# Four graph layers on one core: how the two 8-head attention layers end, and what the stages behind them find ready

## The chip, the core and the metric

The kernel runs on one core of a Trainium2 chip. The core has a matrix engine (PE; its weight loads are listed apart as PEld), a vector engine (DVE), an activation engine (ACT), a general engine (POOL) and a queue engine (SP), and 16 DMA engines that all of them share. PE multiplies out of SBUF into PSUM; DVE and ACT take results from there. DMAs are issued by SP and POOL, a few by ACT, and each of these issues its transfers in its own order. The metric is the device time of one execution in microseconds, the median of the runs.

## What is computed

The input is a matrix `x` of 3327 nodes by 512 features and an adjacency matrix `adj` of 3327 by 3327. Four layers follow one another, each of the form `x = layernorm(x + layer(x, adj))`:

```python
def _L0_gnn_ref(h, adj, W, a):            # layer 0: 8 heads of 64
    Wh = jnp.einsum('ni,hio->hno', h, W)
    f1 = jnp.einsum('hno,ho->hn', Wh, a1)
    f2 = jnp.einsum('hno,ho->hn', Wh, a2)
    e = jax.nn.leaky_relu(f1[:, :, None] + f2[:, None, :], ALPHA)
    attention = jax.nn.softmax(jnp.where(adj[None] > 0, e, NEG_INF), axis=-1)
    h_prime = jnp.einsum('hnm,hmo->hno', attention, Wh)
    ...
def _L1_gnn_ref(X, A, W_nb, b_nb, W_line, b_line, neibor_num):   # layer 1: the first 64 neighbours
    Ab = A > 0
    keep = Ab & (jnp.cumsum(Ab.astype(jnp.int32), axis=1) <= neibor_num)
    cnt = keep.sum(axis=1, keepdims=True).astype(X.dtype)
    nb_mean = (keep.astype(X.dtype) @ X) / jnp.maximum(cnt, 1.0)
    xj = jax.nn.leaky_relu(nb_mean @ W_nb.T + b_nb)
    xi = jax.nn.leaky_relu(X @ W_line.T + b_line)
    return xi + jnp.where(cnt > 0, xj, jnp.zeros((), X.dtype))
```

Layer 2 is again an attention with 8 heads of 64, with an elu behind it, and layer 3 one with 4 heads of 128 and an elu. Layer 1 is called SAGE below.

## The kernel before

The nodes are 26 tiles of 128 rows. Everything that PE does stands in an order written by hand; the instructions of the other engines are ordered by a scheduler with priorities, apart from those that `tc.keep_in_program_order` pins. Tiles come from pools with a fixed number of buffers, so a new tile waits until the users of the old one in its buffer are done. The adjacency, as 0 and 1 in one byte each, stays in SBUF as `mask` for all layers.

**Projection.** For each tile, `project1` transposes x (L258, copied by ACT in L259 to xT) and `project2` multiplies it with the weights (pw, L268), scales the result on DVE (vt, L274) and stores it. In layer 0 this runs while the adjacency comes in (`raw`, made to `mask` in L593). `rows` (L356) loads one row of scores per head and repeats it over 128 partitions (rb); `mean` (L283) adds the row that nodes without neighbours use.

**Attention.** The 26 tiles of results are two halves of 13, and a half has four units of two heads each (of one head in layer 3). A unit goes over 26 tiles j of neighbours. For each j and head, DVE forms t of 128 by 1664 (L402), ACT a sigmoid y of it (L405), and PE multiplies t with the values vj (po, L425) and y with pieces of the denominators (pd, L377, issued in pairs by `den`, three j's behind). A unit's jobs are run in the next unit, one per j: `transposed` (L450) turns ob, the copy of po, by PE, ACT copies the result to hb (L457), and SP stores it to hd in DRAM. After the fourth unit of a half the pieces in pd are added up: four transposes on DVE to db (L486, L487), two reductions to red (L491), four stores to dd in DRAM (L495) in pieces of 32 bytes, one load back in another layout (pes, L498), and `finish_sums` (L501) forms the reciprocals `rec`. A second way (from L522) copies pd to db by ACT and DVE and lets PE add by 13 matmuls (`sums`, L533), with `reciprocals` behind it; before the change only the very last unit of the kernel uses it.

**Counts.** `count_jobs` counts each node's neighbours by PE during layer 0. Its step `none` copies the counts out of PSUM (ct, L629), adds them up (pn, L631), stores them to ctd, and marks the nodes without neighbours (nb, L635).

**Between the layers.** `finish_steps` loads a group of two tiles of h (hd) and of the residual input (xr), divides by the denominators, applies elu, adds, and takes the norm (`norm_rows`: square root on ACT L154, the scaled copy L161). The first group of the next stage is finished inside the attention's end, by `ending`. `sage` has two phases: first projections of each tile (transposes L682, pz L690, pi L693, results as three bf16 parts, two kept in SBUF as zs, the third stored to zd), then sums over neighbours: pk (L770) counts along the neighbours, starting from a carry (cy, L659, copied to PSUM in L762), kt (L774) is the mask cut at 64, and acc (L809) sums over 26 tiles times three parts, the third read back as zl. `third` holds layer 3, with its own projection in groups of two tiles.

## Time and profile before

The three runs took 3410.44, 3410.56 and 3414.77 us; the median is 3410.56. The profiled execution took 3407.9 us, its span is 3406.2.

| engine | busy us | share of the span | instructions |
|---|---|---|---|
| PE | 3262.8 | 96% | 18423 |
| DVE | 2695.3 | 79% | 2630 |
| ACT | 2351.4 | 69% | 2128 |
| POOL | 214.7 | 6% | 344 |

| stage, from the trace | us from the span's start |
|---|---|
| layer 0, projection (adjacency comes in) | 0 to 143 |
| layer 0, attention | 143 to 957 |
| SAGE, projections | 960 to 1180 |
| SAGE, sums over neighbours, projection of layer 2 | 1180 to 1772 |
| layer 2, attention | 1772 to 2562 |
| layer 3 | 2562 to 3406 |

A line of the timeline or of a group names the line of the code, the engine, the operation, what is written and what is read, and the number of instructions; in brackets it tells how long the engine stood idle before it and what ended the wait. A wait line names the waiting instruction, what released it, the sum in us, how often, and the longest. Matmuls are pipelined, so the time between the starts of two lines is a better measure than the busy time of one.

### The profile page before, as it was taken

How to read it: one execution, taken by the hardware profiler on the slowest of the kernel's cores; microseconds unless marked ns; L12 is line 12 of the kernel's file. 1: busy time of each engine (PE TensorE's matmuls, PEld its weight loads, DVE VectorE, ACT ScalarE, POOL GpSimd, SP SyncE). 2: the span in 40 equal slices, each digit the busy share in tenths (PEclk: the TensorE clock that was granted, in tenths of full speed). 3: DMA queues.
4: the chain of work that ended last, by engine and by line, in shares of the span. 5: the costliest groups of instructions: out<-in, count | busy, mean ns of one | idle time of the engine just before them, and what ended most of it. 6: DMA issues, size and time to landing. Idle time of an engine off the chain costs nothing.

```text
span 3406.2 us, 47019 instructions
## 1 busy us (share of the span) xinstructions
PE 3262.8 (96%) x18423; PEld 1631.0 (48%) x18423; DVE 2695.3 (79%) x2630; ACT 2351.4 (69%) x2128; POOL 214.7 (6%) x344
## 2 busy tenths in 40 slices
PE   8899999999989899999989999999997999999997
PEld 7544344444434345555544444444445754445453
DVE  5799999999967544444449999999997766668886
ACT  2388999999943233333338999899996755559885
POOL 3100000000010111111110000000001000000000
PEclk9899999999989999999999999999998999999998
DMA  9544111110143443333320111211107411122311
GB/s 372 214 127 123 52 49 53 42 49 28 38 123 128 116 111 87 90 85 85 85 81 26 41 50 48 56 44 47 35 25 225 169 41 42 41 51 79 95 42 48
DMA packets 313365, 284.65 MB, mean 84 GB/s; under 512 B 134253, under 2 KB 248631, under 8 KB 313144
## 3 DMA queue, kind: packets, MB, share of 16 engines
q1 hardware_dynamic: 280584, 170.27, 16.9%
q0 software_dynamic: 27040, 103.70, 9.5%
q10 hardware_dynamic: 5520, 7.69, 0.7%
q8 instruction: 145, 2.38, 0.3%
q14 instruction: 76, 0.62, 0.1%
HBM read 212.22 MB, written 69.35 MB: 83 GB/s over the span
## 4 chain that ended last, share of the span: by engine, by line
PE 79%; issue 7%; DVE 6%; DMA 4%; ACT 2%; POOL 0%; SPq 0%; ACTq 0%; POOLq 0%; DVEq 0%
PE po L425 49%; PE acc L809 9%; PE pd L377 7%; PE pw L268 5%; DVE t L402 4%; PE pz L690 3%; PE pi L693 3%; DMA raw<-in_adjT_dram 2%; ACT y L405 1%; PE pt L453 1%; DMA cy<-ctd 1%; PE pk L770 1%; PE pt L258 0%; PE pa L1022 0%; DVE mask L593 0%
## 5 line engine op out<-in xcount | busy, mean ns | idle before, releaser
L402 DVE SCALAR_TENSOR_TENSOR t<-rb,qc,mask 128x1664 f32<-128x1664 f32 x1040 | 1959.9, 1957 | 167.7 <-PE po L425 150.1
L405 ACT ACTIVATE y<-t,bi,sc 128x1664 fp8e4<-128x1664 f32 x1040 | 1771.1, 1766 | 317.3 <-PE pd L377 304.4
L425 PE MATMUL po<-t,vj 128*64 128x448 f32 (+3 forms) x8320 | 1924.6, 520 | 25.0 <-DVE t L402 22.3
L425 PEld LDWEIGHTS po<-t,vj 128*64 128x64 f32 (+1 forms) x8320 | 848.3, 148 | 978.2 <-issue 689.7
L809 PE MATMUL acc<-zs,kt 128*128 128x512 bf16 x1352 | 405.1, 382 | 0.0
L809 PEld LDWEIGHTS <-kt 128*128 128x128 fp8e4 x2028 | 199.1, 98 | 250.8 <-issue 9.5
L268 PE MATMUL pw<-wsb,xT 128*128 128x264 f32 (+1 forms) x1248 | 299.8, 395 | 9.2 <-DVE vt L274 7.5
L762 ACT CAST pk<-cy 128x512 f32<-128x512 bf16 x169 | 98.9, 587 | 294.5 <-DVE kt L774 251.1
L377 PE MATMUL pd<-y,sden 128*32 128x448 fp8e4 (+1 forms) x4160 | 259.4, 342 | 8.2 <-ACT y L405 8.2
L268 PEld LDWEIGHTS pw<-wsb,xT 128*128 128x128 f32 x1248 | 240.4, 196 | 53.4 <-issue 5.0
L809 PE MATMUL acc<-zl,kt 128*128 128x512 bf16 x676 | 257.8, 381 | 4.0 <-DMA zl<-zd 4.0
L774 DVE SCALAR_TENSOR_TENSOR kt<-pk,mask 128x512 fp8e4<-128x512 f32 x169 | 116.0, 687 | 99.7 <-PE pk L770 99.7
L377 PEld LDWEIGHTS <-sden 128*32 128x32 bf16 x4160 | 117.6, 96 | 160.3 <-issue 137.6
L274 DVE TENSOR_TENSOR vt<-pw,dc 128x256 f32<-128x256 f32 x156 | 59.0, 418 | 141.2 <-ACT dc L269 137.1
L356 POOL DMA_DIRECT2D rb<-r x40 | 21.9, 548 | 1617.0 <-DVE t L402 1604.5
L272 ACT COPY rc<-pw 128x8 f32<-128x8 f32 (+1 forms) x78 | 12.7, 163 | 138.7 <-PE pw L268 136.2
L690 PE MATMUL pz<-wn,xT 128*128 128x512 f32 x208 | 97.4, 613 | 10.1 <-ACT xT L684 10.1
L693 PE MATMUL pi<-wl,xT 128*128 128x512 f32 x208 | 93.5, 592 | 0.0
L659 POOL DMA_DIRECT2D cy<-ctd x91 | 67.9, 746 | 338.4 <-ACT pk L762 310.2
L782 DVE SCALAR_TENSOR_TENSOR y<-acc,cnt,bnb 128x512 f32<-128x512 f32 x26 | 19.5, 751 | 85.9 <-PE acc L809 85.9
L593 DVE TENSOR_SCALAR mask<-raw 128x832 fp8e4<-128x832 int32 (+2 forms) x90 | 53.1, 598 | 40.4 <-DMA raw<-in_adjT_dram 40.1
L154 ACT ACT_TABLE_LOAD x45 | 57.7, 1283 | 37.3 <-DVE mv L153 36.7
(177 smaller groups left out, 1661.6 us busy)
## 6 DMA issues: line engine op xcount, KB each, us to landing
vj<-v SPq DMA_DIRECT2D x312, 128.0 KB
rb<-r POOLq DMA_DIRECT2D x40, 832.0 KB, 4.6
raw<-in_adjT_dram SPq DMA_DIRECT2D x67, 416.0 KB
cy<-ctd POOLq DMA_DIRECT2D x78, 256.0 KB, 3.9
h<-hd SPq DMA_DIRECT2D x61, 256.0 KB
v<-vt SPq DMA_DIRECT2D x50, 256.0 KB
hd<-hb SPq DMA_DIRECT2D x48, 256.0 KB
xr<-x POOLq DMA_DIRECT2D x45, 256.0 KB, 3.2
```

The source lines that it names most:

```text
L268: nc.tensor.matmul(pw[e][:, :FW + H], xT[:, c, :], wsb[:, c, e, :], start=c == 0, stop=c == FC - 1)
L274: nc.vector.tensor_tensor(vt[:, hs, :], pw[e][:, :FW].rearrange("p (h d) -> p h d", d=D), self.dc[:, t, hs].rearrange("p (h e) -> p h e", e=1)
L377: nc.tensor.matmul(pd[c][32 * kk:32 * kk + 32, :w_], lhsT, rhs, start=(kk, c) not in seen, skip_group_check=final is not None, stop=last a ...
L402: nc.vector.scalar_tensor_tensor(t, rb[k], self.qc[:, j, h:h + 1], mask[:, j, i0:i0 + IW], op0=ALU.max, op1=ALU.mult)
L405: nc.scalar.activation(y, t, AF.Sigmoid, bias=self.bi[:, j, h:h + 1], scale=self.sc[:, j, h:h + 1], saturate=False)
L425: nc.tensor.matmul(po[c][k * D:(k + 1) * D, :z - a_], vj[:, j % 2, k * D:(k + 1) * D], ts[k][:, a_:z], start=j == 0, stop=j == NT - 1)
L659: nc.gpsimd.dma_start(out=cy[:, :n, :], in_=ctd[t:t + n, b * GW:(b + 1) * GW] .rearrange("(o t) i -> o t i", o=1).to_broadcast([P, n, GW]))
L690: nc.tensor.matmul(pz, xT[:, c, :], wn[:, c, :], start=c == 0, stop=c == FC - 1)
L693: nc.tensor.matmul(pi, xT[:, c, :], wl[:, c, :], start=c == 0, stop=c == FC - 1)
L762: nc.scalar.copy(pks[k % 2], carry[b, t // 4 * 4][:, t % 4:t % 4 + 2, :])
L774: nc.vector.scalar_tensor_tensor(kt, pk, NEIGHBOURS, mask[:, t:t + 2, i0:i0 + GW], op0=ALU.is_le, op1=ALU.mult, saturate=False)
L809: nc.tensor.matmul(acc, kts[t][:, s * P:(s + 1) * P], zs(t, c) if c < 2 else zl[:, t, :], start=t == 0 and c == 0, stop=t == NT - 1 and c ...
```

## The change

The diff has five parts.

1. The half boundary of the 8-head layers takes the second way of adding up (`by_pe`): ACT copies pd, PE adds, DVE multiplies and takes reciprocals; the result lies in a bank of its own.
2. Where the first way stays (the ends of the 8-head layers, and layer 3), red is stored to dd in one piece per partition, and `place` loads it back in 16 pieces, from a job of its own. At the end of an 8-head layer `place` and `finish_sums` are put off into the next stage (`self.late`), where they run at tiles 4 and 8, with the loads on SP; in layer 3 the loads are on POOL. rec is first filled with a copy of rc.
3. At the ends of these layers, the last hb tiles, xr and e use buffers of other tiles (vj, db, hb).
4. In SAGE, two carries are loaded ahead and the pool has three; the next group of tiles is finished after the first transposes of a group; the count row cb and its reciprocals move to the first phase; the first sum takes all zl matmuls behind the others, and the weights wsb are loaded after it, by SP. `third` loads wsb after the first group and finishes the next group later in the same way.
5. In layer 0, xt has five buffers instead of three, the first rows are loaded later, and in `none` the copy of the counts goes to ACT, and the comparison reads the SBUF copy.

```diff
@@ finish_steps
-                xr = pool.tile([P, F], F32, name="xr", bufs=xbufs)
+                xr = xpool.tile([P, F], F32, name="xr", tag="hb") if xpool else \
+                    pool.tile([P, F], F32, name="xr", bufs=xbufs)
...
@@ unit
-                ending()
+                ending(sp)
             den(NT - 2, late)
...
-                hb = sp.tile([P, 4, P], F32, name="hb")
+                if HS == 2 and half == 1 and s == NS - 1 and n < 4:
+                    hb = vp.tile([P, n, P], F32, name="hb", tag="vj")
+                elif HS == 2 and half == 1 and s == NS - 1 and s0 >= 8:
+                    hb = sp.tile([P, 4, P], F32, name="hb", tag="db", bufs=1)
+                else:
+                    hb = sp.tile([P, 4, P], F32, name="hb")
...
-            if not (final and s == NS - 1):
+            by_pe = HS == 2 and half == 0 or final and s == NS - 1
+            if not by_pe:
+                end = half == 1 and s == NS - 1
...
-                dd = dram.tile([IW, 2, 2 * NS], F32, name=f"dd{self.li}{half}{s}")
-                for kk in range(4):
-                    i_, w_ = (0, WA) if kk < 2 else (WA, WB)
-                    nc.sync.dma_start(out=dd[i_:i_ + w_, kk % 2, :].rearrange("(b i) x -> i b x", i=32),
-                                      in_=red[32 * kk:32 * kk + 32, :w_ // 32].rearrange("p b o s -> p b (o s)"))
-                pes = sp.tile([P, HALF, 2, 2, NS], F32, name="pes", tag="red", bufs=1)
-                nc.sync.dma_start(out=pes.rearrange("p q k o s -> p q (k o s)"),
-                                  in_=dd.rearrange("(q p) k x -> p q (k x)", p=P))
+                dd = dram.tile([P, WA // 32, 2 * NS], F32, name=f"dd{self.li}{half}{s}")
+                nc.sync.dma_start(out=dd, in_=red.rearrange("p b o s -> p b (o s)"))
+                held = []
+                def place(pool=sp, tag="red", eng=nc.gpsimd):
+                    pes = pool.tile([P, HALF, 2, 2, NS], F32, name="pes", tag=tag, bufs=1)
+                    held.append(pes)
+                    for kk in range(4):
+                        q0, nq = (0, NA) if kk < 2 else (NA, HALF - NA)
+                        src = dd[32 * kk:32 * kk + 32, :4 * nq].rearrange("i (q m) x -> m i q x", m=4)
+                        for m in range(4):
+                            eng.dma_start(out=pes[32 * m:32 * m + 32, q0:q0 + nq, kk % 2]
+                                          .rearrange("p q o s -> p q (o s)"), in_=src[m])
+                nc.vector.tensor_copy(rec[:, t0:t0 + HALF, hs], self.rc[:, t0:t0 + HALF, hs])
...
+                if end:
+                    self.late = [lambda pool: place(pool, "pes", nc.sync), lambda pool: finish_sums()]
+                    return jobs
...
             for c in range(2):
                 nc.scalar.copy(db[:64, c * (WA // 2):(c + 1) * (WA // 2)], pd[c][:64, :WA // 2])
-                nc.vector.tensor_copy(db[64:, c * (WB // 2):(c + 1) * (WB // 2)], pd[c][64:, :WB // 2])
+                (nc.scalar.copy if HS == 2 else nc.vector.tensor_copy)(
+                    db[64:, c * (WB // 2):(c + 1) * (WB // 2)], pd[c][64:, :WB // 2])
...
-                pe = po[0][:, :2 * HALF * H].rearrange("p (q o h) -> p q o h", q=HALF, o=2)
+                pe = po[0][:, :2 * HALF * H].rearrange("p (q o h) -> p q o h", q=HALF, o=2) if final else \
+                    qp.tile([P, HALF, 2, H], F32, name="pe", tag="q")
...
+            if not final:
+                return jobs[:2] + [sums, nothing, reciprocals] + jobs[2:]
@@ count_jobs, none
-                nc.vector.tensor_copy(ct[:, :w_], held["p"][:, :w_])
+                nc.scalar.copy(ct[:, :w_], held["p"][:, :w_])
...
-                nc.vector.tensor_scalar(nb[:, :w_], pn[:, :w_], 0.0, None, op0=ALU.is_equal, saturate=False)
+                nc.vector.tensor_scalar(nb[:, :w_], ct[:, :w_], 0.0, None, op0=ALU.is_equal, saturate=False)
@@ sage
-                tc.tile_pool(name="sg_c", bufs=2, reuse_waits="tile") as cyp:
+                tc.tile_pool(name="sg_c", bufs=3, reuse_waits="tile") as cyp:
...
+            load_carry()
             load_carry()
...
+                cb = zp.tile([P, NT], BF, name="cb")
+                nc.gpsimd.dma_start(out=cb, in_=ctd[NT:NT + 1, :].rearrange("o (t p) -> p (o t)", p=P))
+                cnt = zp.tile([P, 3, NT], F32, name="cnt")
...
-                    ys, ahead = ahead, finish(fp, xin, prev, t0 + 2, 2, 6, nc.sync if t0 else nc.gpsimd) \
-                        if t0 + 2 < NT else None
+                    ys = ahead
+                    if t0 in (4, 8):
+                        prev.late.pop(0)(fp)
+                    if t0 == 8:
+                        tc.keep_in_program_order(
+                            nc.vector.tensor_scalar(cnt[:, 0, :], cb, NEIGHBOURS, 1.0, op0=ALU.min, op1=ALU.max))
+                        nc.vector.reciprocal(cnt[:, 1, :], cnt[:, 0, :])
+                        nc.vector.tensor_scalar(cnt[:, 2, :], cb, 0.0, None, op0=ALU.is_gt)
                     for s, y in enumerate(ys):
                         xT = step1(y)
+                        if s == 0 and t0 + 2 < NT:
+                            ahead = finish(fp, xin, prev, t0 + 2, 2, 6, nc.sync if t0 else nc.gpsimd)
...
-                load_wide(wsb, wsrc, nc.gpsimd)
-                nc.vector.tensor_copy(wsb[:, :, :, FW:], wa[nxt.li].rearrange("p c (e h) -> p c e h", e=2))
...
-                            for c in range(3):
+                            for c in range(2 if t0 + s == 0 else 3):
...
+                        if t0 + s == 0:
+                            for t in range(NT):
+                                nc.tensor.matmul(acc, kts[t][:, :P], zl[:, t, :], start=False, stop=t == NT - 1)
+                            load_wide(wsb, wsrc, nc.sync)
+                            tc.keep_in_program_order(nc.vector.tensor_copy(
+                                wsb[:, :, :, FW:], wa[nxt.li].rearrange("p c (e h) -> p c e h", e=2)))
@@ third
-                load_wide(wsb, w3, nc.gpsimd)
-                nc.vector.tensor_copy(wsb[:, :, :, FW:], wa[3].rearrange("p c (e h) -> p c e h", e=2))
...
-                for t0 in (2, 4):
-                    load_group(t0)
+                load_group(2)
+                load_wide(wsb, w3, nc.gpsimd)
+                nc.vector.tensor_copy(wsb[:, :, :, FW:], wa[3].rearrange("p c (e h) -> p c e h", e=2))
+                load_group(4)
                 for t0 in range(0, NT, 2):
                     ys = ahead
+                    if t0 in (4, 8):
+                        L2.late.pop(0)(fp)
                     load_group(t0 + 6)
-                    if groups:
-                        ahead, steps = groups.pop(0)
-                        for f in steps:
-                            f()
                     for s, y in enumerate(ys):
...
                         xT = L3.project1(pp, ps, y, t)
+                        if s == 0 and groups:
+                            ahead, steps = groups.pop(0)
+                            for f in steps:
+                                f()
@@ layer 0, projection
-                xt = pp.tile([P, F], F32, name="xt")
+                xt = pp.tile([P, F], F32, name="xt", bufs=5)
...
                     L0.prepare(pp, 0)
+                    L0.cut(pp, 0)
+                if t == NT - 6:
                     L0.first_rows = L0.rows(rp, 0, 0)
-                    L0.cut(pp, 0)
```

## The prediction

> **What bounds the kernel now.** I read the busy time by stage first, because the busy shares of the whole span average over stages with different limits.
>
> ```profile
> 143.00:960.00 817.00, 794.11 (x5786) 343.76 (x5787) 812.00 (x503) 742.85 (x497) 9.73 (x18) 0.99 0.20 61
> 960.00:1180.00 220.00, 199.98 (x546) 93.42 (x546) 140.91 (x268) 72.97 (x127) 20.62 (x36) 0.95 0.39 123
> 1180.00:1210.00 30.00, 25.30 (x98) 10.56 (x98) 9.52 (x17) 6.34 (x11) 6.53 (x9) 0.85 0.78 210
> 1772.00:2562.00 790.00, 776.16 (x5508) 352.30 (x5510) 786.14 (x455) 733.95 (x487) 11.34 (x19) 0.99 0.14 41
> 2562.00:2700.00 138.00, 112.50 (x552) 94.24 (x545) 110.06 (x265) 98.52 (x204) 17.70 (x33) 0.91 0.67 221
> ```
>
> Columns: stretch, length, busy time of PE, weight load, DVE, ACT and POOL, then the granted TensorE clock, DMA share, GB/s. In the attention of the two 8-head layers (143 to 960, 1772 to 2562) DVE has no room (812 of 817, 786 of 790 us): there every DVE microsecond saved is time. In the stages after them PE should be the bound, but loses 20, 5 and 25 us and some clock. Before 127 us the DMAs are full with the adjacency; the last four-head layer is PE's. The timeline of PE shows where the loss at the end of layer 0 sits, that of SP why:
>
> ```profile
> 964.19 1.36 PE L682 MATMUL pt<-ident,h 128*128 128x128 f32 x8 [1.17 <-ACT h L161]
> 975.61 6.38 PE L690 MATMUL pz<-wn,xT 128*128 128x512 f32 x8 [10.06 <-ACT xT L684]
> 981.83 3.60 PE L693 MATMUL pi<-wl,xT 128*128 128x512 f32 x8
> 988.31 1.11 PE L682 MATMUL pt<-ident,h 128*128 128x128 f32 x4 [2.89 <-ACT h L161]
> 989.22 4.62 PE L690 MATMUL pz<-wn,xT 128*128 128x512 f32 x8
> ...
> 964.19 10.69 SPq L495 DMA_DIRECT2D dd<-red  x4
> 974.98 1.02 SPq L458 DMA_DIRECT2D hd<-hb  x2
> ```
>
> ACT copies xT late because it stands behind an hb copy (9.45 us idle); hb's two buffers are freed by stores that SP issues only after four dd stores, 10.69 us. The waits at the other two places:
>
> ```profile
> PE pk L770 <- ACT pk L762: 5.6, 3, 3.6
> PE acc L809 <- DMA zl<-zd: 4.0, 1, 4.0
> ...
> 2575.44 1.97 PE L258 MATMUL pt<-ident,h 128*128 128x128 f32 x8 [10.61 <-DMA xr<-x]
> 2577.28 4.34 PE L268 MATMUL pw<-wsb,xT 128*128 128x260 f32 x16
> 2590.47 1.12 PE L258 MATMUL pt<-ident,h 128*128 128x128 f32 x4 [8.85 <-ACT h L161]
> 2591.38 5.73 PE L268 MATMUL pw<-wsb,xT 128*128 128x260 f32 x16
> 2597.39 3.67 PE L268 MATMUL pw<-wsb,xT 128*128 128x260 f32 x16
> ```
>
> **The change, part by part.**
>
> *Projection of layer 0: 0 (−7.5 to +1).* More xt buffers and later row loads would remove PE's one stall there, 5.83 us at 109.5, with about 1.6 of slow clock. But the stage ends on the adjacency: its last piece is set at 127.2, the last projection follows at 128.3, the mean at 142.9. That cover gone, the gain is 7.5.
>
> *Counts: −4 (−6 to 0).* Eight times, the copy out of PSUM (L629) leaves DVE for ACT: six of 512 columns spaced 0.60, two of 128 spaced 0.20, so 6×0.60+2×0.20 = 4.0. The comparison (L635, also 0.60) reads SBUF instead of PSUM; the trace has no such form, so I bound it by nothing saved and by the mask row from SBUF (L593, mean 0.598, mostly 832 columns), scaled to 0.37 for 512: 6×0.23, with the short ones 1.6, saved in all. Against it: ACT's copy (0.57) queues behind a sigmoid (1.77), so PE waits 1.3 to 2 each time, four times per unit, with the matmuls of the next heads behind it; PE needs 3.40 of 3.73 us per pair, 8.5 us slack per unit, less 5 to 8 for the waits. I take two thirds of 5.6.
>
> *Half boundary of both 8-head layers: −2.4 each (−3.3 to +0.5).* DVE's four transposes and two reductions go:
>
> ```profile
> 2171.79 0.64 DVE L486 STREAM_TRANSPOSE db<-pd 64x448 f32<-64x448 f32 x1
> 2172.45 0.59 DVE L487 STREAM_TRANSPOSE db<-pd 64x384 f32<-64x384 f32 x1
> ...
> 2176.19 0.98 DVE L491 TENSOR_REDUCE red<-db 128x112 f32<-128x336 f32 x2
> ```
>
> 2171.79 to 2174.32 is 2.53, 2176.19 to 2177.07 is 0.88: 3.41. ACT takes four copies of about 0.5 (the last layer's form), PE 13 fp32 matmuls, 3.06 us by their row at the end; ACT has 5 us of room in a unit of 96.85, PE 8.5. With six t buffers I let 1 us come back.
>
> *End of layer 0 and start of SAGE: −2.8 (−7 to +2).* The dd stores become one of 128 long pieces, hb gets other buffers (vj's and db's), so the first pz comes at an estimated 967.5 instead of 975.6. But what is late next is the second pair of tiles. The last sigmoid now stands behind the square root and two table loads of 1.28: +2.1, so y ends at 962.2, and the wn/wl loads, which wait for it, move too. POOL then has to issue two carries, wn, wl, blb and the count row cb (2-byte pieces; the same load took 2.4 us in before, 1188.36 to 1190.79) ahead of the second pair's h and x; the second x also waits for an hb store. They land at an estimated 975 to 977 (before: 971 to 973). DVE's comparison of cb, not pinned, can sit in front of that pair, and 17 DVE operations of the first tiles come ahead of its norm: pt of tile 2 at about 985.5 instead of 988.3. So 8 us of stall is moved, not removed. Here a rule bears. The rows: pz took 6.38 after 10.06 us of idleness, pi directly after 3.60, and after 2.89 us still 4.62. The Trainium skill, TensorE: Matmul & The Clock Gate, Part 1 (the HAM clock gate), says that an idle window of about 3.4 us halves the clock and that it takes as long a busy one to come back. By the rule the short gap would cost nothing but itself, by the row 1.0 more. Both say that a moved gap of 8 us pays its slow start again; counting the early pz as full-speed would add 2.8 of gain. I leave it out.
>
> *The placing.* Sixteen loads of 192 to 224 pieces of 32 bytes (3,328 in all) stand in the next stage on SP, eight ahead of one pair's h loads, eight ahead of a later pair's. The Trainium skill, DMA: Bandwidth & Descriptors, Why small descriptors are slow, adds 32 bytes of description to each, so the change's small pieces are only moved from stores to loads. By the page (3,328×64 bytes at its 435 GB/s) that is an estimated 0.5 us; by the rows, 10.69 and 8.12 us for as many 32-byte pieces, it is 8 to 11 us of SP's time per stage. I take the row. It is hidden by h tiles loaded a pair ahead (a pair is some 15 us of PE in SAGE's projections); uncovered, 8 to 11. The reciprocals that wait for it are pinned on DVE; everything behind them waits, but the order puts two pairs between. An added copy of rc is about 0.2.
>
> *SAGE's two phases: −9 (−12 to −5).* Before, PE waits for zl (3.96 at 1181.1) and for the carry (3.57 at 1192.6): the carry load landed at 1191.76 behind 1 MB of wsb (1187.2), bnb (1188.4) and cb (1190.8); three small gaps make 2.4 more, and the matmuls go at 0.43 instead of 0.22 us apart for some 10 us (clock 0.85). First acc tile over at 1207.4. After: zl is read last, wsb goes after that tile, three carries are there. The tile's work from 1176.1 is 78 acc at 0.216 and 13 pk at about 0.18, 19.2, so 1195.3, plus 3 of slow clock: 9 earlier. If the zl matmuls still wait it is 5.
>
> *End of layer 2: −11 (−14 to −6).* hb no longer waits (2.37+2.38), wsb's megabyte moves behind the first x and h (the h that DVE waits 3.57 for landed at 2572.7, wsb at 2570.1 and 2572.1), and DVE's wait for pes, 5.85 at 2583, goes. Worked along the chain h, norm, transpose: first pw at 2572.3 (was 2577.3), third tile's transposes 2580.2 (2590.5), fifth's 2591 (2602.5). Less than all of the 20 us of gaps, as norms switch tables twice per pair.
>
> *Last layer: 0 (−1 to +2).* Its placing is on POOL, else idle, and DVE is busy 508 of 706 us.
>
> Sum: 0 − 4 − 2×2.4 − 2.8 − 9 − 11 = −31.6. The profiled execution took 3407.9 (span 3406.2), so 3376.3; the runs' median lies 2.7 above that execution: 3379.0.
>
> **Rivals.** *Half the gain, 3394.* The stalls move on: at SAGE's start to the second and third pair behind POOL's queue (0 instead of −2.8), at layer 2's end to the third pair behind the placing (−6), counts swallowed by PE's waits (0), boundaries −5 and −1.2 each: −13.4 to −17. For it: the POOL order above and ACT's table loads. Against: layer 2's POOL queue is short.
> *More, 3367.* The projection was set by xt (−7.5) and SAGE's start gives −7. Against: adjacency pieces land to the end.
> *No change.* Attention limited by PE and ACT, and each gap reappearing elsewhere. Against it DVE at 812 of 817, and that wsb, bnb and cb leave the carry's way for good.
> *Slower, 3440.* The small loads cost per load, not per piece: each of the four dd stores took 2.67, and 16 at that price are 42.7 us of SP in each of two stages. About 11 are covered, 2×31.7 = 63 lost: +32. It decides (slower than before by 0.2%) from 1.9 us per load on, (38.4/2+11)/16. Against: SP's h loads, of 128 pieces, take 0.5 each.
>
> **How the numbers follow.** Likeliest 0.60 (its own range 3367 to 3391); half 0.20; more 0.08; nothing 0.04; slower 0.08. About 0.2%, 6.8 us, is what a measurement tells from no change. The range 3361 to 3402 takes in the half and most of the more. Faster 0.88, same 0.04, slower 0.08.
>
> **What would show it.** Right: no 10 us gap in front of the first pz, PE waits of zl and pk under 2 us, first acc tile done some 19 to 22 us after it began, the two gaps at layer 2's end under 5 us each, half boundaries with no DVE transposes at an unbroken 1.86 us spacing. Wrong: a new gap over 10 us at pt of tiles 2 to 6 with h or pes as releaser, placing loads over 1 us each on SP, DVE idle in a unit with counts.

## The result, and the profile after

The changed kernel takes 3392.35 us, the median of four runs (3386.22 to 3395.04). The kernel before, run beside it, takes 3411.16 us. The ratio is 0.994, with an interval of 0.9923 to 0.9957. The kernel is faster by 18.8 us, where the forecast said 31.6. The profiled execution took 3391.7 us (before 3407.9), with a span of 3390.0.

The busy time by stage, of the changed kernel; the columns are those of the prediction's first view:

```profile
143.00:960.00 817.00, 791.82 (x5838) 340.95 (x5837) 805.79 (x496) 752.87 (x518) 13.27 (x22) 0.99 0.20 62
960.00:1180.00 220.00, 198.80 (x541) 92.35 (x540) 141.98 (x267) 72.83 (x123) 19.24 (x35) 0.95 0.40 120
1180.00:1210.00 30.00, 26.69 (x110) 11.42 (x110) 11.39 (x21) 8.34 (x15) 5.81 (x8) 0.89 0.71 222
1772.00:2562.00 790.00, 775.98 (x5551) 352.12 (x5549) 786.17 (x459) 738.77 (x497) 16.66 (x28) 0.99 0.14 43
2562.00:2700.00 138.00, 122.08 (x579) 101.36 (x580) 113.06 (x282) 105.89 (x214) 13.03 (x24) 0.94 0.62 211
```

The windows are fixed in time while the work has moved forward, so the rows tell only where to look. The second row has as much lost PE time as before: 198.80 busy, where it was 199.98. The start of SAGE has not been mended. PE's timeline there, then SP's and POOL's:

```profile
957.00 0.54 PE L378 MATMUL pd<-y,sden 128*32 128x448 fp8e4 x6 [3.08 <-ACT y L406]
962.25 3.70 PE L722 MATMUL pz<-wn,xT 128*128 128x512 f32 x8 [1.69 <-ACT xT L716]
965.79 3.60 PE L725 MATMUL pi<-wl,xT 128*128 128x512 f32 x8
986.41 1.12 PE L714 MATMUL pt<-ident,h 128*128 128x128 f32 x4 [17.02 <-ACT h L161]
987.32 4.93 PE L722 MATMUL pz<-wn,xT 128*128 128x512 f32 x8
...
961.07 0.33 SPq L505 DMA_DIRECT2D dd<-red  x1
970.18 5.15 SPq L515 DMA_DIRECT2D pes<-dd  x8
976.49 5.72 SPq L515 DMA_DIRECT2D pes<-dd  x8
...
958.52 1.49 POOL L741 DMA_DIRECT2D cb<-ctd  x1
971.00 0.55 POOL L126 DMA_DIRECT2D xr<-in_x_dram  x1 [10.43 <-issue]
```

The 10 us in front of the first pz have shrunk to 1.69, and dd takes SP 0.33 us instead of 10.69. But 17.02 us now stand in front of the second pair's transposes, where 2.89 stood. The first xr of the second pair is issued at 971.00. The waits of PE at SAGE's first sum, and PE's timeline there and at the end of layer 2:

```profile
PE pk L805 <- ACT pk L797: 4.9, 3, 3.2
...
1185.56 0.58 PE L805 MATMUL pk<-mask,upto 128*128 128x512 fp8e4 x1 [3.20 <-ACT pk L797]
1185.94 1.91 PE L845 MATMUL acc<-zs,kt 128*128 128x512 bf16 x4
...
2563.18 1.97 PE L259 MATMUL pt<-ident,h 128*128 128x128 f32 x8 [4.96 <-ACT h L161]
2565.36 4.54 PE L269 MATMUL pw<-wsb,xT 128*128 128x260 f32 x16 [0.21 <-ACT xT L260]
2576.06 1.12 PE L259 MATMUL pt<-ident,h 128*128 128x128 f32 x4 [6.16 <-ACT h L161]
2576.97 5.47 PE L269 MATMUL pw<-wsb,xT 128*128 128x260 f32 x16
```

The wait for zl is gone. The one for the carry (pk) is not: 3.2 us at its longest, where it was 3.6. At the end of layer 2 the gaps of 10.61 and 8.85 us have become 4.96 and 6.16.

Where the time went shows best when each stage is measured from an event that it doesn't influence to the next one. Times are those of the two profiled executions, one of each kernel. Together the rows give −16.6; the stretches between them make up the rest to the executions' −16.2:

| stretch | before | after | difference | forecast |
|---|---|---|---|---|
| start to the first t of layer 0 | 142.95 | 143.34 | +0.4 | 0 |
| the units of layer 0 that hold the counts (first three) | 321.02 | 318.26 | −2.8 | −4 |
| unit with the half boundary, layer 0 | 101.54 | 98.64 | −2.9 | −2.4 |
| last t of layer 0 to the second pair's transposes | 37.26 | 40.61 | +3.3 | −2.8 |
| SAGE's sums (first acc to last acc) | 577.79 | 573.15 | −4.6 | −9 |
| last acc to the first t of layer 2 | 18.86 | 22.19 | +3.3 | 0 |
| unit with the half boundary, layer 2 | 101.37 | 97.95 | −3.4 | −2.4 |
| last t of layer 2 to the 33rd pw | 42.99 | 34.88 | −8.1 | −11 |
| layer 3, first t to last t | 671.05 | 669.28 | −1.8 | 0 |

### The profile page after: what moved, and what is told of

It is laid out like the page before. It is cut to its first block, busy times and chain, and to the rows that moved or that the text cites. A ratio compares the mean times of both kernels' runs of the same rounds, so it can differ in the third digit from the quotient of the medians.

```text
span 3390.0 us, 47140 instructions
## 1 busy us (share of the span) xinstructions
PE 3248.7 (96%) x18423; PEld 1623.0 (48%) x18475; DVE 2685.2 (79%) x2615; ACT 2357.2 (70%) x2142; POOL 241.7 (7%) x390
## 4 chain that ended last, share of the span: by engine, by line
PE 84%; DVE 4%; issue 4%; DMA 4%; ACT 3%; POOL 0%; ACTq 0%; POOLq 0%; DVEq 0%; SPq 0%
PE po L426 50%; PE acc L845 12%; PE pd L378 7%; PE pw L269 5%; DVE t L403 3%; PE pz L722 3%; PE pi L725 3%; DMA raw<-in_adjT_dram 2%; ACT y L406 1%; PE pk L805 1%; PE pt L454 1%; DMA asb<-in_a_dram 0%; PE pa L1066 0%; PE pt L259 0%; PE pt L714 0%
## 5 line engine op out<-in xcount | busy, mean ns | idle before, releaser
L426 PEld LDWEIGHTS po<-t,vj 128*64 128x64 f32 (+1 forms) x8320 | 836.1, 148 | 974.5 <-issue 702.3
L845 PE MATMUL acc<-zs,kt 128*128 128x512 bf16 x1312 | 395.1, 382 | 2.2 <-issue 0.2
L845 PE MATMUL acc<-zl,kt 128*128 128x512 bf16 x638 | 241.8, 379 | 0.6
L357 POOL DMA_DIRECT2D rb<-r x40 | 21.7, 544 | 1685.7 <-DVE t L403 1664.4
L273 ACT COPY rc<-pw 128x8 f32<-128x8 f32 (+1 forms) x78 | 12.7, 163 | 155.5 <-PE pw L269 152.9
```

The costliest lines, as they stand in the source:

```text
L426: nc.tensor.matmul(po[c][k * D:(k + 1) * D, :z - a_], vj[:, j % 2, k * D:(k + 1) * D], ts[k][:, a_:z], start=j == 0, stop=j == NT - 1)
L845: nc.tensor.matmul(acc, kts[t][:, s * P:(s + 1) * P], zs(t, c) if c < 2 else zl[:, t, :], start=t == 0 and c == 0, stop=t == NT - 1 and c ...
```

## The experiments

After the result the theory was this. The gap at the second pair has several causes in a row: the load of cb, scattered in pieces of 2 bytes, a division on DVE that waits for the third pair's h, and a last sigmoid that comes late. The first sum waits because the 3.4 MB of zl fill the DMA engines ahead of the carry. Layer 2 starts late because cb's place in memory moved the order of DVE's work. The rival: the gap is the price of the sixteen placing loads on SP, and the first sum is limited by the clock alone.

All diffs are against the changed kernel. The first t of layer 0 falls between 141.6 and 145.4 us from run to run, so the readings are distances inside an execution. "Pair" is the distance from the last t of layer 0 to the second pair's transposes, "sum" that from the first acc to the first sum's last one, "start" that from the last acc to the first t of layer 2. These three are read from one execution of each run. Seven of the twelve medians lie within the scatter of the changed kernel's four runs; e12's interval is the only one that lies wholly below the changed kernel's, and e6's the only one wholly above.

| run | median us (runs) | before beside it | ratio, interval | pair | sum | start |
|---|---|---|---|---|---|---|
| changed kernel | 3392.35 (4) | 3411.16 | 0.994, 0.9923–0.9957 | 40.61 | 27.12 | 22.19 |
| e1_cb_late | 3390.78 (4) | 3410.12 | 0.9942, 0.9928–0.9957 | 37.56 | 23.88 | 22.38 |
| e2_place_late | 3390.11 (4) | 3410.12 | 0.994, 0.9925–0.9954 | 37.71 | 24.08 | 22.41 |
| e3_zl_paced | 3393.13 (4) | 3410.12 | 0.9951, 0.9936–0.9966 | 40.47 | 27.12 | 22.17 |
| e4_counts_dve | 3394.05 (4) | 3410.12 | 0.9953, 0.9936–0.997 | 40.42 | 25.94 | 21.85 |
| e5_cb_old | 3396.91 (7) | 3407.95 | 0.9967, 0.9956–0.9978 | 37.37 | 33.62 | 19.92 |
| e6_pin_divide | 3436.75 (4) | 3407.95 | 1.0087, 1.0071–1.0104 | 36.97 | 25.71 | 22.35 |
| e7_zl_paced | 3387.83 (4) | 3407.95 | 0.9947, 0.9932–0.9961 | 40.52 | 20.95 | 21.97 |
| e8_half_dve | 3389.66 (4) | 3407.95 | 0.9952, 0.9937–0.9967 | 35.65 | 24.09 | 22.20 |
| e9_joined | 3386.98 (5) | 3411.11 | 0.9928, 0.9914–0.9941 | 35.54 | 23.72 | 20.06 |
| e10_joined2 | 3381.94 (5) | 3410.11 | 0.9913, 0.9899–0.9926 | 35.31 | 21.66 | 20.08 |
| e11_y_first | 3383.74 (4) | 3408.19 | 0.9926, 0.991–0.9943 | 34.15 | 23.52 | 21.70 |
| e12_joined3 | 3375.86 (4) | 3408.19 | 0.9906, 0.9891–0.992 | 32.20 | 21.02 | 19.7 |

### What makes the gap at SAGE's second pair

DVE's timeline of the changed kernel in the gap, with what it waited for in brackets:

```profile
968.71 0.18 DVE L753 TENSOR_SCALAR cnt<-cb 128x26 f32<-128x26 bf16 x1 [7.67 <-DMA cb<-ctd]
974.27 0.69 DVE L195 TENSOR_TENSOR h<-h,xr 128x512 f32<-128x512 f32 x1 [4.14 <-DMA xr<-in_x_dram]
977.01 0.68 DVE L195 TENSOR_TENSOR h<-h,xr 128x512 f32<-128x512 f32 x1
980.97 0.69 DVE L181 TENSOR_TENSOR h<-h,rec 128x512 f32<-128x512 f32 x1 [3.27 <-DMA h<-hd]
981.58 0.69 DVE L152 BATCH_NORM_STATS2 st<-h 128x6 f32<-128x512 f32 x1
```

There are three waits. The first is for cb, the second for the second pair's xr. The third is a division of the *third* pair, whose h was issued on SP behind eight placing loads. It stands in front of the second pair's statistics (L152), which had all they needed at about 977.7. DVE takes its instructions in order, so the second pair waits for the third one's transfer.

**e1**: cb is loaded two groups later, and its comparison is pinned.

```diff
-                nc.gpsimd.dma_start(out=cb, in_=ctd[NT:NT + 1, :].rearrange("o (t p) -> p (o t)", p=P))
...
+                    if t0 == 4:
+                        tc.keep_in_program_order(nc.gpsimd.dma_start(
+                            out=cb, in_=ctd[NT:NT + 1, :].rearrange("o (t p) -> p (o t)", p=P)))
...
-                        nc.vector.tensor_scalar(cnt[:, 2, :], cb, 0.0, None, op0=ALU.is_gt)
+                        tc.keep_in_program_order(
+                            nc.vector.tensor_scalar(cnt[:, 2, :], cb, 0.0, None, op0=ALU.is_gt))
```

> The changed kernel, with the load of the count row cb (3,328 pieces of 2 bytes) moved from the start of SAGE's projections to the third group of tiles, and its comparison pinned there. Theory A (these pieces fill the DMA queues from 958.5 to 968.7 and make the second pair's h and xr late): the 17.0 us gap ahead of the transposes of tile 2 shrinks by 4 to 7, to 10 to 13; the whole about 5 us (0.15%) faster than the changed kernel. Theory B (the gap is made by the 16 pes loads on SP, which delay the h loads of the third pair that DVE takes in front of the second pair's norm): gap 16 to 17, no change. Theory C (the second pair waits for the memory of the attention's last hb, whose store ends late anyway): gap 16 to 17, no change.

The pair comes at 37.56 instead of 40.61. Measured from the last t, the addition of the xr is 1.9 us earlier, and the division's wait is 2.17 instead of 3.27. PE's gap is still 13.88. So cb's load costs 3 us here, and is one cause of several; the gap left is more than the 10 to 13 us expected. The packets of the DMAs show how. Those of the attention's last hb stores end 22.9 us after the last t instead of 24.9, and the second pair's first xr, which waits for memory that these stores free, is issued at 23.3 instead of 25.2. The same holds in e5, e9 and e10, where cb isn't loaded here either. The median moves by less than the runs scatter.

**e2**: the placing loads come two tiles later, at tiles 6 and 10, in both `sage` and `third`, and are pinned on SP.

```diff
-                    if t0 in (4, 8):
+                    if t0 in (6, 10):
...
-                            eng.dma_start(out=pes[32 * m:32 * m + 32, q0:q0 + nq, kk % 2]
+                            ins = eng.dma_start(out=pes[32 * m:32 * m + 32, q0:q0 + nq, kk % 2]
...
+                            if tag == "pes":
+                                tc.keep_in_program_order(ins)
```

> The changed kernel, with the 16 pes loads one group of tiles later (issued at tile 6 instead of 4, the reciprocals at tile 10 instead of 8) and pinned behind the h loads before them, in SAGE's projections and in layer 3's. Theory B: at SAGE's start the h of tile 4 is there 5 us earlier, DVE's wait of 3.27 us for it goes, and the 17.0 us gap falls to 12 to 14. Theory A or C: gap 16 to 17. At layer 2's end, where eleven of the loads run from 2572 to 2578.7, behind the second pair's h: no change of the gaps of 4.96 and 6.16 us by any of them (1 us either way).

The pair comes at 37.71, 2.9 earlier, and the division's wait of 3.27 is gone, so the placing loads delayed the third pair's h, and by DVE's order the second pair. At the end of layer 2 nothing is gained (gaps 4.95 and 6.64), and layer 3's projection, from the last t of layer 2 to the first of layer 3, is 134.45 instead of 133.21. The rival that the placing loads are the whole gap falls: 14.10 us of it are left without them.

**e6**: the division is pinned in program order, in both stages.

```diff
-            nc.vector.tensor_tensor(h.rearrange("p (h d) -> p h d", h=H), h.rearrange("p (h d) -> p h d", h=H),
+            ins = nc.vector.tensor_tensor(h.rearrange("p (h d) -> p h d", h=H), h.rearrange("p (h d) -> p h d", h=H),
...
+            if pin:
+                tc.keep_in_program_order(ins)
```

> The changed kernel, with the division of each group (L181) pinned in DVE's program order in SAGE's projections and in layer 3's, so that the third pair's division no longer stands ahead of the second pair's norm. Theory E (DVE takes the third pair's division first and waits for its h: 3.27 us at SAGE's start, 3.43 at layer 2's end, with the second pair's norm queued behind): the gap of 17.0 us falls to 13 to 15 and that of 6.16 to 2.5 to 4. Rival (the second pair's own transfers are late): both stay within 1 us. Later groups: no change, PE bounds there.

At SAGE's start this is right: the pair comes at 36.97, 3.6 earlier. The kernel as a whole is slower than before. The waits of PE in layer 3's projection (us in total, times, longest), first in e6, then in the changed kernel:

```profile
PE pt L261 <- ACT h L161: 48.7, 13, 5.7
```

```profile
PE pt L259 <- ACT h L161: 14.5, 4, 6.2
```

Every pair now waits. A pinned division can't be placed ahead of its program position; that the scheduler had fetched it forward for the later pairs, and that this is what was lost, is the reading of these waits. The projection takes 48 us more. The freedom that costs 3 us at one pair is worth 48 over layer 3's projection. Nor did the second gap at layer 2's end close (5.09).

**e11**: the square root of the first norm is pinned behind the attention's last sigmoid (`behind` is set only for the group that is finished at the end of layer 0).

```diff
-        nc.scalar.activation(rs[:, :n, 0], mv[:, :n, 1], AF.Sqrt, bias=eps)
+        ins = nc.scalar.activation(rs[:, :n, 0], mv[:, :n, 1], AF.Sqrt, bias=eps)
+        if behind:
+            tc.keep_in_program_order(ins)
```

> The changed kernel, with the square root of the first two tiles' norm pinned behind layer 0's last sigmoid on ACT (before the change it stood there too; in the changed kernel it and a table load stand ahead of it, and PE waits 3.08 us for that sigmoid instead of 0.93). The prediction's step (+2.1 us at this place): that wait falls to 0.5 to 1, the wn and wl loads, which wait for the sigmoid, and the reductions come 2 to 3 us earlier, and with them the second pair: 37 to 39 us from the last t to the transposes of tile 2 instead of 40.6. Rival (the second pair hangs on the memory that the attention's last stores free, and on the DMAs' bytes, which start no earlier): the wait falls but the 40.6 stays within 1 us.

ACT's timeline of the changed kernel shows the two table loads around that square root, ahead of the last sigmoid; PE's of e11 shows the wait for that sigmoid, which was 3.08, and the gap:

```profile
952.27 1.28 ACT L154 ACT_TABLE_LOAD   x1
953.88 1.28 ACT L406 ACT_TABLE_LOAD   x1
955.17 1.77 ACT L406 ACTIVATE y<-t,bi,sc 128x1664 fp8e4<-128x1664 f32 x1
```

```profile
954.72 0.54 PE L380 MATMUL pd<-y,sden 128*32 128x448 fp8e4 x6 [0.92 <-ACT y L408]
979.80 1.12 PE L716 MATMUL pt<-ident,h 128*128 128x128 f32 x4 [10.96 <-ACT h L163]
```

The wait falls from 3.08 to 0.92: 2.2 us, which the prediction had put at 2.1. The pair comes 6.5 us earlier, more than that and more than expected. The pin moved DVE's order too, as its timeline in e11 shows:

```profile
972.74 0.69 DVE L197 TENSOR_TENSOR h<-h,xr 128x512 f32<-128x512 f32 x1 [4.23 <-DMA xr<-in_x_dram]
976.17 0.69 DVE L152 BATCH_NORM_STATS2 st<-h 128x6 f32<-128x512 f32 x1
977.45 0.66 DVE L183 TENSOR_TENSOR h<-h,rec 128x512 f32<-128x512 f32 x1
```

The third pair's division now stands behind the second pair's statistics, and waits for nothing. This run changed two things and can't divide the rest between them.

### What the first sum waits for

**e3** and **e7**: the thirteen loads of zl go from SP, where they are issued in one stretch of 14.31 us, to POOL, one for each two tiles of the first sum. In e3 wsb stays on SP; in e7 it follows the last zl on POOL.

```diff
-                for t in range(0, NT, 2):
-                    nc.sync.dma_start(out=zl[:, t:t + 2, :], in_=zd[t * P:(t + 2) * P, :]
-                                      .rearrange("(t p) f -> p t f", p=P))
...
+                            if t0 + s == 0 and t % 2 == 0:
+                                tc.keep_in_program_order(nc.gpsimd.dma_start(
+                                    out=zl[:, t:t + 2, :], in_=zd[t * P:(t + 2) * P, :]
+                                    .rearrange("(t p) f -> p t f", p=P)))
```

e7 has this in addition:

```diff
-                            load_wide(wsb, wsrc, nc.sync)
+                            for e in range(2):
+                                tc.keep_in_program_order(nc.gpsimd.dma_start(
+                                    out=wsb[:, :, e, :FW],
+                                    in_=wsrc[:, e * FW:(e + 1) * FW].rearrange("(c p) m -> p c m", p=P)))
```

> The changed kernel, with the 13 zl loads (3.4 MB) no longer issued at once on SP at the start of the sums over neighbours, but one by one on POOL behind the carries, along the first sum. Theory A (zl's bytes share the DMA engines with the carry that PE waits for: cy issued 1176.1, landed 1184.8): the 3.20 us wait of pk for the carry goes, and with it the half clock of some 6 us after it; the first sum ends 4 to 6 us earlier than 1201.4, whole kernel 4 to 6 us (0.15%) faster than the changed kernel. Theory B (the carry is late because it waits for its buffer, three being too few): the wait stays at 3 us, and with POOL's issue of 0.55 us per zl load in front of each carry the sum ends the same or 1 to 3 us later.

> As the run with zl paced on POOL, now with wsb's megabyte held behind the last zl load, on POOL (in that run its issue moved up to 1173.9 and took zl's place). Theory A (bytes in front of the carry): the pk wait of 3.2 us falls under 1.5, and the first sum takes 21 to 24 us from its first acc to the 78th instead of 27.1. Theory B (each carry starts only when its buffer is free, and takes 5.9 us to land even on quiet queues): the wait stays at 2.5 to 3.5.

e3 settles nothing: wsb, not pinned on SP and no longer behind zl there, was issued at 1173.89, and its megabyte took zl's place ahead of the carry. The sum took 27.12 as before, with a wait of 3.44. e7 removes that, and its waits and timeline of PE read:

```profile
PE pk L802 <- ACT pk L794: 1.7, 2, 1.2
...
1185.53 1.02 PE L846 MATMUL acc<-zs,kt 128*128 128x512 bf16 x4
```

The long wait is gone and the sum takes 20.95, 6.2 less (about half of it the wait and half a slow clock behind it, as the last section shows), inside the 19 to 22 that the prediction had named for a sum without these waits. So the carry waited for the bytes of zl. That the clock alone limits the sum is refuted; it comes on top.

**e5**: cb, its load and its reciprocals go back to the second phase, with the weights.

```diff
                 nc.gpsimd.dma_start(out=bnb, in_=bn.to_broadcast([P, F]))
+                cb = wp.tile([P, NT], BF, name="cb")
+                nc.gpsimd.dma_start(out=cb, in_=ctd[NT:NT + 1, :].rearrange("o (t p) -> p (o t)", p=P))
...
-                cb = zp.tile([P, NT], BF, name="cb")
-                nc.gpsimd.dma_start(out=cb, in_=ctd[NT:NT + 1, :].rearrange("o (t p) -> p (o t)", p=P))
```

> The changed kernel, with the count row cb, its load and the three operations on it back in the second phase of SAGE, as in the kernel before. Theory A (cb's 2-byte pieces cost the second pair at SAGE's start about 3 us, as with the later load): from the last t of layer 0 to the transposes of tile 2 37 to 38 us instead of 40.6. Theory D (the 3.3 us lost between the last acc and the first t of layer 2 come from cb's new buffer: with it in the longer-lived pool the scheduler puts the first casts of `cut` behind the last vt, 23 operations between that vt and the first t instead of 16): that stretch falls from 22.2 to 18.5 to 20 us; rival (the slow clock of the last projection alone): it stays at 21 to 22.4. The first sum over neighbours gets cb's load back: 1 to 4 us longer than the changed kernel's 27.1. Whole: 1 to 5 us faster than the changed kernel.

Three readings come out of it. The pair is at 37.37, which confirms e1. The carry, now behind cb as well as zl, makes PE wait 9.62 instead of 3.20, and the sum takes 33.62:

```profile
1185.61 0.59 PE L803 MATMUL pk<-mask,upto 128*128 128x512 fp8e4 x1 [9.62 <-ACT pk L795]
```

So it was right to take cb out of the second phase. The sum loses 6.5 us, where 1 to 4 were expected, and the whole is not faster, as expected, but slower (3396.91 us). And layer 2 starts 19.92 us after the last acc instead of 22.19.

### Why layer 2 starts later

DVE's timeline between the last two tiles' vt and the first t, of the kernel before and then of the changed one (rows between left out):

```profile
1763.94 0.39 DVE L332 CAST pc<-dc 128x104 bf16<-128x104 f32 x1
...
1768.62 0.76 DVE L274 TENSOR_TENSOR vt<-pw,dc 128x256 f32<-128x256 f32 x2 [2.56 <-ACT dc L269]
...
1772.77 11.26 DVE L402 SCALAR_TENSOR_TENSOR t<-rb,qc,mask 128x1664 f32<-128x1664 f32 x6
```

```profile
1763.09 0.76 DVE L275 TENSOR_TENSOR vt<-pw,dc 128x256 f32<-128x256 f32 x2 [5.40 <-ACT dc L270]
1764.72 0.33 DVE L333 CAST pc<-dc 128x104 bf16<-128x104 f32 x1
```

Before, seven operations that cut the scores into pieces stand ahead of the last vt, where DVE waits anyway (16 operations from there to the first t). After, all stand behind it (23), and the wait is 5.40 instead of 2.56. The distance from the row of these vt to the first t grows from 4.15 to 6.50 us. No line of the change touches this code. e5, e9, e10 and e12, which have cb in another pool than the changed kernel, have the 16 operations again and start at 19.7 to 20.1; the eight others, e1 among them, which loads cb later but leaves it in its pool, have 23 and start at 21.7 to 22.4. So the order goes with the pool that cb lies in, though no run moves the pool alone; how the scheduler comes to it was not looked into. Of the remaining 1.0 us, 0.8 is the last tile's projection (pw), which takes 6.12 us instead of 5.32.

### Counts and half boundaries

**e4**: the copy of the counts goes back to DVE, and the comparison stays on SBUF.

```diff
-                nc.scalar.copy(ct[:, :w_], held["p"][:, :w_])
+                nc.vector.tensor_copy(ct[:, :w_], held["p"][:, :w_])
```

> The changed kernel, with the copy of the counts back on DVE (the comparison still reads the SBUF copy). Prediction's theory (ACT's copy saves DVE 4.0 us in all but gives some back through PE's waits): the units with counts in layer 0 (first and third) are together 1 to 3 us longer than in the changed kernel, second unit unchanged. Rival (the copy on ACT delays y and through it the next unit: the second unit became 1.06 us longer than before): first plus third 3 to 4 us longer, second 1 us shorter, sum about +2. If ACT's copy gained nothing at all, the sum of the first three units is within 0.5 us of the changed kernel's 318.3.

The first three units take 320.86 instead of 318.26 us, and the third, which holds four counts, 102.62 instead of 100.90. The copy is worth 1.7 of the 2.0 us that it occupied DVE for in that unit, which takes 100.9 in all twelve executions with the copy on ACT. The first unit is no such measure: it takes 112.6 to 114.6 in those twelve. The second unit, 101.93 before, takes 102.5 to 103.0 in every variant, with 102.81 in e4, so its growth isn't due to the copy on ACT. DVE now waits there 0.25 to 0.73 us for pieces of the adjacency, and did not before; the rest was not traced. The rows of the comparison, before and after (minimum, median and maximum in ns), show what reading the copy in SBUF saves:

```profile
L635 DVE TENSOR_SCALAR nb<-pn x8: 284/680/682, 181.2 to 441.4; 128x512 fp8e4<-128x512 f32 x6, 128x128 fp8e4<-128x128 f32 x2
```

```profile
L666 DVE TENSOR_SCALAR nb<-ct x8: 219/420/427, 183.2 to 441.0; 128x512 fp8e4<-128x512 bf16 x6, 128x128 fp8e4<-128x128 bf16 x2
```

That is 0.26 us each, six times, and 0.065 twice: 1.7 in all, where the prediction estimated 1.6.

**e8**: the half boundaries take the first way again.

```diff
-            by_pe = HS == 2 and half == 0 or final and s == NS - 1
+            by_pe = final and s == NS - 1
```

> The changed kernel, with the sums at the half boundary of both 8-head layers back on DVE's transposes and reductions (stored to dd and placed from there by POOL). Theory of the prediction (DVE saves 3.41 us, something comes back): the first unit of the second half is 2.4 to 3.5 us longer in both layers, 101 to 101.5 instead of 97.9 to 99.6; the whole 5 to 7 us slower than the changed kernel. Rival (the placing by 16 loads and the four extra operations are what matter): 0 to 2 us.

The units of the half boundaries take 101.52 and 101.40, 2.9 and 3.45 more, as expected. In layer 2 this is clear: the twelve executions with the second way take 97.9 to 98.1. In layer 0 they take 98.6 to 99.7, and e6, without an edit there, 101.23, so the gain there is less sure than one pair of executions tells. The whole isn't slower, which was missed: at SAGE's start the pair comes 5.0 earlier, and the first sum is 3.0 shorter behind nearly the same wait (3.29). Two things differ at SAGE's start: cb is issued 14.4 instead of 12.7 us after the last t, and the second pair's first xr 22.5 instead of 25.2. The first row is POOL's, the second DVE's:

```profile
961.82 1.50 POOL L741 DMA_DIRECT2D cb<-ctd  x1 [1.64 <-issue]
...
972.89 0.69 DVE L195 TENSOR_TENSOR h<-h,xr 128x512 f32<-128x512 f32 x1 [0.84 <-DMA xr<-in_x_dram]
```

The addition of xr waits 0.84 instead of 4.14. That cb's later issue let the stores that xr waits for go first is likely, but not tested; and why POOL stood 1.64 us before that issue, some 400 us after the edit's sixteen loads, was not found.

### The causes joined

**e9** joins e7 with a later placing in SAGE (as in e2) and cb in the second phase behind zl. **e10** instead keeps cb in the first phase, late as in e1, but in the pool of the carries (so does cnt; the line below). **e12** adds e11's pin to e10.

```diff
-                cb = zp.tile([P, NT], BF, name="cb")
+                cb = cyp.tile([P, NT], BF, name="cb", bufs=1)
```

> The changed kernel with three repairs: zl one by one behind the carries and wsb after them (as in the run that did this), cb back in the second phase but loaded only after the last zl load, and SAGE's pes loads one group later, pinned behind the h loads. If the causes named so far are the whole of what the change gave away between the layers, the sum is: SAGE's start 3 + 3 us (from the last t to the transposes of tile 2 34 to 35 instead of 40.6), the first sum 5 to 6 us (21 to 22 instead of 27.1), the last acc to the first t of layer 2 2.3 us (20 instead of 22.2): 12 to 15 us faster than the changed kernel, 3377 to 3381. Rival (the causes at SAGE's start overlap: either repair alone uncovers the other's wait, since the second pair's xr waits for the attention's memory in any case): SAGE's start 3 us in all, the whole 9 to 11 us. If cb's pieces now hold up the carries of the second block, the second sum loses up to 6 us again.

> As the joined kernel before, with cb loaded at the third group of SAGE's projections instead of between the two phases' loads, and cb and its reciprocals in the carries' pool (which leaves the order of the casts ahead of layer 2 as in the kernel before). If cb's pieces were what made the second sum's carry late in the joined kernel (2.41 us of pk wait and half clock after it, 6.6 us in all between the first sum's end and the last), that stretch falls back from 552.6 to 546 to 548; SAGE's start stays at 35 to 36 us, the first sum at 21 to 24, the start of layer 2 at 20: 3376 to 3382 in all. Rival (the other carries, or the weights behind zl, made it late): that stretch stays at 550 to 553, the whole at 3385 to 3388.

> The second joined kernel with the same pin: if the pin helps there as well, from the last t to the transposes of tile 2 33 to 34 us instead of 35.3, the whole 3378 to 3381; if not, 35 to 36 and 3380 to 3384.

e9's pair and start are as e10's, but it loses 5 us later, and so misses its 3377 to 3381: from the first sum's end to the last acc it takes 552.63 instead of 546.03. PE waits 2.41 us for the second block's carry at 1197.3. In e10, with cb loaded earlier, that wait is gone and the stretch takes 547.77, as expected if cb had held up the carry.

e12 is the fastest, and faster than expected: 3375.86 us, 32.3 less than the kernel before beside it. Its pair comes at 32.20, with 8.85 us of gap left:

```profile
977.69 1.11 PE L718 MATMUL pt<-ident,h 128*128 128x128 f32 x4 [8.85 <-ACT h L163]
```

That is about the 31.6 of the forecast, reached with edits that the forecast didn't have: they move work that stood in front of something more urgent, and cb and cnt into another pool.

## Why the prediction was right or wrong

The direction, the range and the shape were right; the likeliest time was 13 us too low. The result lies by the rival "half the gain" (3394), whose sentence on SAGE's start, that the stall moves on to the second pair, is what happened, though its own terms were off: it had nothing from the counts and 6 at layer 2's end.

- *Projection of layer 0* (0): right, +0.4 in one execution, below its scatter from run to run.
- *Counts* (−4, measured −2.8): the two rates were right: the copy gives 1.7 of 2.0 in the unit with four counts, the comparison saves 1.7 in all. What comes back was charged at a third of the gain, for waits of PE behind a sigmoid. Such waits show in the first unit: DVE stands 0.4 to 0.7 us for a sigmoid there in eight of the twelve executions with the copy on ACT, and not in e4. Two terms were missed: the second unit, 0.6 to 1.1 longer, and a wait behind the very first t, put down to the store of the mean row. The kernel before doesn't have it, every changed one has it, with 0.6 to 1.05 us:

```profile
145.95 5.68 DVE L403 SCALAR_TENSOR_TENSOR t<-rb,qc,mask 128x1664 f32<-128x1664 f32 x3 [0.66 <-DMA v<-ms]
```

  The three units take 316.1 to 318.4 us in those twelve, 2.6 to 4.9 less than in the one execution of the kernel before. So the −4 isn't refuted, and the −2.8 is one draw.
- *Half boundary* (−2.4, measured −2.9 and −3.4): the 3.41 us of DVE's transposes and reductions were right. In layer 2 nothing of the 1 us "let come back" did: DVE forms 17 t in 31.75 us, one every 1.87, straight through the boundary. In layer 0 it waits 0.44 us for PE, and in seven of the other eleven executions with the second way a further 1 us; there the 1 us was about right.
- *End of layer 0 and start of SAGE* (−2.8, measured +3.3): **the step that failed most.** The mechanism, 8 us of stall moved and not removed, was named with its parts: the sigmoid late by 2.1, cb in front, the second xr. The size was wrong because the parts were folded into one estimate of when POOL's queue would be through. Two things were missing in it. cb's load was costed at 2.4 us, the distance between two landings in the kernel before; it took 10.2 us from issue to landing, and the stores and loads beside it were late with it (3 us, e1 and e5). And the third pair's division, ahead of the second pair's norm and behind eight placing loads (3 to 3.6 us, e2 and e6), was in no step: I said of the placing that "the order puts two pairs between", which holds for the reciprocals and not for the h loads queued behind the placing on SP. With both mended (e10) the stretch takes 35.3 us, 2.0 less than before, where 2.8 less was forecast.
- *The placing*: its price came out right by luck. Sixteen loads take 10.87 us of SP, inside the 8 to 11 taken from the dd stores at the ends of the layers, as if these were the price of 3,328 pieces. They aren't: at the half boundary of layer 0 the kernel before stores as many pieces in a fifth of the 10.69 us,

```profile
573.83 2.08 SPq L495 DMA_DIRECT2D dd<-red  x4
```

  so most of the 10.69 was SP standing for another reason, which was not tested. The sixteen loads cost 0.64 to 0.72 us each on average, and 9.34 us together on POOL in layer 3. That is far below the 1.9 from which "slower" would have decided. What the placing was hidden by was wrong.
- *SAGE's two phases* (−9, measured −4.6): zl no longer makes PE wait and wsb no longer delays the carry, but the carry still stands behind zl's 3.4 MB: one issued at 1176.12 landed at 1184.84. I moved zl's matmuls behind the others and left its bytes in front. (bnb stays in front of that carry too, though the prediction has it leave.) Without zl's bytes (e7) the sum takes 20.95. Of the 27.12 us measured, the wait for the carry is 3.2 and another 3.2 bad luck with the clock: e1, e2 and e8 have the same wait and take 24 us. With their clock the term would have been about −7.8.
- *Last acc to layer 2* (nothing said, measured +3.3): no step had it. The order of DVE's instructions there went with the pool that cb lies in (2.3), and a projection was slower (0.8).
- *End of layer 2* (−11, measured −8.1): the first pw comes 17.5 us after the last t, where 17.9 was worked out. The second pair is 2.4 late: its gap is 6.16 instead of under 5. It is 5.1 to 7.3 in every variant, also in e2, where the placing comes later, so the placing isn't what sets it. What does stays open.
- *Last layer* (0, measured −1.8): not a gain that can be counted. The stretch takes 669.1 to 669.4 us in eight of the variants, but 671.0 to 671.2 in e5, e8 and e11, whose layer 3 is the same, so 2 us come and go there.

Of the signs named for a wrong prediction one came true: a gap of over 10 us at the second pair, with h as its releaser. Of those named for a right one, the first pz without a 10 us gap came, and the boundary without transposes; the waits under 2 us, the first sum of 19 to 22 us and a second gap under 5 us at layer 2's end did not.

Open are, besides, the last 9 us of the gap in e12: the second pair's second xr waits for memory that the attention's last hb store frees, and for the bytes of wl, hb and h; neither was taken away by itself.

## What to carry to other kernels

Where a load is moved out of one critical place, write down what stands behind it in its new queue, up to the landing and not only to the issue: here a 6.5 KB row and eight small loads each moved a stall rather than removing it. On an engine that works in order, look for an operation of a later group, waiting for a late transfer, in front of an earlier group's work; move its transfer, or pin the operation in that one place: pinned for every group, it saved 3.6 us in SAGE and cost 48 in layer 3. And moving the matmuls that read a large load doesn't help a small one queued behind its bytes: pace the large one, and see that no other takes its place.

## What the runs showed of the hardware

The smallest load was among the slowest. The DMA issues of the changed kernel between 955 and 975 us (size, and us from issue to landing) have cb, one row that is scattered over 128 partitions in pieces of 2 bytes, at 10.2 us, and a carry 40 times as large at half of that:

```profile
cy<-ctd POOLq DMA_DIRECT2D x1, 256.0 KB, 5.1
...
cb<-ctd POOLq DMA_DIRECT2D x1, 6.5 KB, 10.2
```

In the kernel before it took 11.5. Not all of this is cb's own: it stands behind two loads, 1.25 MB together, on the same queue, the second of which landed 4.4 us before it. Issued later, in e1, e10 and e12, it takes 6.4 to 7.3 us. Its neighbours pay as well: in e1 a 256 KB load of xr takes 3.2 us just before cb, 6.3 and 5.9 beside it, and 2.8 behind it. That agrees in its direction with what the prediction cites from the Trainium skill, DMA: Bandwidth & Descriptors, Why small descriptors are slow. But the records show cb as 64 packets of 128 and 32 bytes, not as 3,328 of 2, so that the pieces are the cause is not shown.

An equal gap can cost 3 us more or nothing. The first sum of the changed kernel and that of e1 have the same wait (3.20 and 3.03 us). The ten microseconds after 1180, with the granted clock in the third column from the right, for the changed kernel and then for e1:

```profile
1180.00:1190.00 10.00, 6.80 (x22) 2.56 (x21) 2.83 (x5) 2.88 (x5) 1.59 (x3) 0.73 1.08 343
```

```profile
1180.00:1190.00 10.00, 6.92 (x33) 3.08 (x32) 3.65 (x7) 2.88 (x5) 2.27 (x3) 1.00 1.08 332
```

Behind the wait, four acc matmuls take 1.91 us in the changed kernel, whose clock has a mean of 0.73 over these ten microseconds, and 1.03 in e1, at 1.00. In e2 and e8, with slightly longer waits (3.25 and 3.29), the sums were again 24.08 and 24.09; in e3, with 3.44, it was 27.12. The Trainium skill, TensorE: Matmul & The Clock Gate, Part 1 (the HAM clock gate), says that the activity window runs freely and the count of slow matmuls so varies from run to run. The rows agree, and give its price here: the sums of 27.12 and 23.88 differ by 3.2 us at equal waits. A gain of 3 us in one profile can therefore be the clock's, and was not counted as an edit's.
